# A decoder layer on one core: both layernorm quarters between the halves of the output's products

## The chip, the cores and the metric

The kernel runs on one core of one Trainium2 chip. The time is the device time of one execution in microseconds (us). A core has five engines that run side by side, each through its own queue in order: TensorE (PE in the profile; its weight loads are listed as PEld), VectorE (DVE), ScalarE (ACT), GpSimd (POOL) and SyncE (SP), which here only issues transfers. An instruction that waits holds back everything behind it in its engine's queue.

## The reference

The input x is 8 batches of 256 rows of 1024 values. The layer is

```
x = x + attn(layernorm(x))          # 32 heads of 32, 8 key/value heads, sign weights
x = x + xattn(layernorm(x), ctx)    # 16 heads, low-rank queries and keys
x = x + ffn(layernorm(x))           # low-rank gate/up and down, silu
```

In the self-attention every projection (q, k, v and the output) is a product with the signs of a weight matrix, scaled per output by the mean of that row's absolute weights and a given factor, and passed through nan_to_num (NaN to 0, infinities to plus or minus 1e6). The scores are softmaxed over 256 keys. All is float32.

## The kernel before, in words

Rows are worked on in tiles of 128, two to a batch (`TB` = 2). The self-attention runs batch by batch in steps: step c (0 to 7) of a batch handles four heads. The cross-attention follows in steps of the same form, then the feed-forward part.

One step, written out by `step` (from L682), does the following, in program order. TensorE makes the scores `s` of four heads (L549) into four PSUM banks of the pool `pss`. VectorE reduces each head's row maximum to `nm` (L692). TensorE transposes the four heads' probabilities of the *step before* in four groups of four (`turned`, L528), each into a PSUM bank from `bank`, and ScalarE copies each group out as `pT` (L532). ScalarE makes the eight exponentials `p` (L711), two to a head, each with its row sum by an accumulator read. At the end TensorE multiplies the turned probabilities with v (`weighted`, L587).

Between the transposes and that last product lie the step's *parts*: pieces of other work that fill TensorE while the softmax is under way. `self_plan(b)` lists the parts for each of the eight steps of batch b, and `run_part` runs one. The parts that matter here are:

- `o_parts`: the output projection of the batch before, one for each row tile and half of the columns. It is a PSUM sum of 16 matmuls (L496) in two halves of 8; after the second half VectorE scales it to `y` (L505), and `nan_to_num` makes `z` and `fin` on VectorE (L355, L358) and `tmp` and a sum on GpSimd (L356, L357). A predicated copy (L361) and the residual sum on GpSimd (L510) follow some parts later.
- `ln_parts`: the layernorm of the next batch, in quarters (row tile and half of the columns). `normed_half` makes `xn` on VectorE ahead of time (L155), four transposes turn it into a PSUM bank (L163), ScalarE copies it as the rounded high part `xh` (L348), and VectorE subtracts to get the rest `xl` (L349), which frees the bank.
- `lnx_parts`: the same for the cross-attention; VectorE alone copies the bank out as `xT` (L847).

Each part has an estimated duration (2.0 for a half of products, 0.5 for a quarter), and `step` adds these up to place the exponentials between the parts on ScalarE: before each part it issues exponentials while their own count (0.49 each) is behind. A row sum becomes a reciprocal on VectorE for two heads at a time (`over_sums`, L562), and the probabilities are divided in place: the letters in `BY` say for each head by whom, D for VectorE (L572, two instructions), P for GpSimd (L565, one) and A for ScalarE (L579, two, issued at the end of the step by `over_sums_end`). ScalarE also rounds the weighted sums to `oh` (L604) at the head of the next step, and VectorE makes the rest `ol` (L608).

`bank` hands out three PSUM banks in turn (one of the pool psB, two of psA). A step with one product and two layernorm quarters takes seven: four turned groups, the product, and the two quarters. So the first turned group of the next step takes the product's bank, the second the first quarter's, the third the second quarter's, and the fourth the first turned group's own, when ScalarE has copied it out.

The order of every engine's queue is the order in which the program issues (a manual schedule). Transfers are issued from SyncE's queue and, for the writes of x1 and x2, from GpSimd's. Deferred work (`later`, `ripe`, `settle`) runs at the start of the following parts, so the number of parts behind a product decides where the predicated copy, the residual sum and the write of x1 (L515) come.

Of the kernel before, what the change touches and what calls it, by code (L numbers as in the profile page):

```python
# [35 lines left out]
def decoder_layer(  # L36
# [25 lines left out]
    B, S, E = x.shape  # L62
# [261 lines left out]
    def scale_part(col0, n, dst, soon=False):  # L324

        box = {}

        def ahead():
            box["dg"] = wk_.tile([P, n, P], F32, tag="xn", name="dg", bufs=2)
            for k in range(n):  # L330
                nc.gpsimd.tensor_scalar_mul(
                    box["dg"][:, k, :], ident, scol[:, col0 + k : col0 + k + 1]
                )

        def main():
            ps = bank([P, n, P], "ps_d")
            for k in range(n):
                nc.tensor.matmul(ps[:, k, :], ones, box["dg"][:, k, :], start=True, stop=True)
            nc.vector.tensor_copy(dst, ps.rearrange("p k c -> p (k c)"))

        return Part(0.3 * n, main, ahead, soon)

    def weight(i):
        return Part(1.1, lambda: weight_next(i))
# [22 lines left out]
    def ln_parts(st, b):  # L367


        def ahead(q):  # L370
            t, h = q // 2, q % 2
            need(st)
            st.xn = getattr(st, "xn", {})
            st.xn[q] = normed_half(xb[b][t], st.mv[:, t, 0:1], st.rs[:, t : t + 1], h)

        def main(q):
            t, h = q // 2, q % 2
            if q == 0:
                st.xh = wk_.tile([P, EC, S], F32R, tag="xh", name="xh")
                st.xl = wk_.tile([P, EC, S], F32R, tag="xl", name="xl")  # L380
            ps = four_T(st.xn.pop(q), "ps_t")
            e4, t4 = slice(h * 4, (h + 1) * 4), slice(t * P, (t + 1) * P)
            split(st.xh[:, e4, t4], st.xl[:, e4, t4], ps)

        return [Part(0.5, lambda q=q: main(q), lambda q=q: ahead(q), True) for q in range(2 * TB)]
# [56 lines left out]
    def q_parts(st, c0):  # L442
        return proj_T(
            st, lambda i, e: qT_w[c0 + i][:, e, :], c0, lambda: st.qT[:, c0 : c0 + 2, :]
        )
# [3 lines left out]
    def k_parts(st):  # L449
        def dst():  # L450
            st.kT = wk_.tile([P, 2, S], F32, tag="kT", name="kT", bufs=2)
            st.qT = wk_.tile([P, EC, S], F32, tag="qT", name="qT", bufs=2)
            return st.kT

        def then():
            nc.vector.tensor_scalar_mul(st.kT, st.kT, K_SCALE)

        return proj_T(st, lambda i, e: kT_w[:, e, i * P : (i + 1) * P], 8, dst, then)

    def v_parts(st):  # L460
        box = {}

        def main(t):
            if t == 0:
                box["ps"] = bank([P, TB, KVD], "ps_v")
                box["y"] = wk_.tile([P, TB, KVD], F32, tag="y", name="y", bufs=2)
            ps, y = box["ps"], box["y"]
            for e in range(EC):
                for x_ in (st.xh, st.xl):
                    nc.tensor.matmul(  # L470
                        ps[:, t, :],
                        x_[:, e, t * P : (t + 1) * P],
                        vT_w[:, e, :],
                        start=(e == 0 and x_ is st.xh),
                        stop=(e == EC - 1 and x_ is st.xl),
                    )
            if t == TB - 1:
                for k in range(TB):
                    nc.vector.tensor_mul(y[:, k, :], ps[:, k, :], v_sc)
                st.v = wk_.tile([P, TB, KVD], F32, tag="v", name="v", bufs=2)  # L480
                nan_to_num(st.v, y, [P, TB, KVD], None)

        return [Part(2.0, lambda t=t: main(t)) for t in range(TB)]
# [306 lines left out]
    def ctx_parts(st, copies):  # L790
        def main(q):
            t, h = q // 2, q % 2
            if q == 0:
                st.cT = wk_.tile([P, EC, S], F32, tag="xh", name="cT")
            ps = four_T(st.c[t][:, h * 512 : (h + 1) * 512], "ps_c")
            copies[h](st.cT[:, h * 4 : (h + 1) * 4, t * P : (t + 1) * P], ps)

        return [Part(0.5, lambda q=q: main(q), hold=True) for q in range(2 * TB)]
# [25 lines left out]
    def ckvT_part(st):  # L824
        def main():
            ps = bank([P, TB, XD], "ps_kt")
            for k in range(TB):
                nc.tensor.transpose(
                    ps[:, k, :], st.ckv[0:XD, k * P : (k + 1) * P], ident[0:XD, 0:XD]
                )  # L830
            nc.vector.tensor_copy(st.ckvT, ps)

        return [Part(0.3, main)]

    def lnx_parts(st):
        def ahead(q):
            t, h = q // 2, q % 2
            need(st)
            st.xn = getattr(st, "xn", {})
            st.xn[q] = normed_half(st.x[t], mv2[st.b][:, t, 0:1], rs2[st.b][:, t : t + 1], h)  # L840

        def main(q):
            t, h = q // 2, q % 2
            if q == 0:
                st.xT = wk_.tile([P, EC, S], F32, tag="xl", name="xT")
            ps = four_T(st.xn.pop(q), "ps_t")
            dve(st.xT[:, h * 4 : (h + 1) * 4, t * P : (t + 1) * P], ps)  # L847

        return [Part(0.5, lambda q=q: main(q), lambda q=q: ahead(q), True) for q in range(2 * TB)]

    def cq_part(st):
        def main():
            ps = bank([P, S], "ps_q")
            for e in range(EC):
                nc.tensor.matmul(  # L855
                    ps, xw.wqd[:, e, :], st.xT[:, e, :], start=(e == 0), stop=(e == EC - 1)
                )
            st.cq = wk_.tile([P, S], F32, tag="v", name="cq", bufs=2)
            nc.vector.tensor_scalar_mul(st.cq, ps, 1.0 / 8.0)

        return [Part(3.5, main)]
# [242 lines left out]
    def tail(fb, j):  # L1104
# [16 lines left out]
    BY = {  # L1121
        0: ["DDDD", "PPPD", "PPPD", "PPPP", "PPPD", "PPPD", "DDDD", "PPPD"],
        1: ["DDAA", "PPAA", "PPAA", "DDDA", "DDAA", "DDDA", "DDDA", "DDDA"],
        B - 1: ["DDAA", "DDDA", "DDDA", "PPAA", "PPAA", "DDDA", "DDDA", "DDDA"],
    }
    sts, xts = [], []
    for b in range(B):
# [6 lines left out]
    def mixed(a, b):  # L1134
        out = []
        for i in range(max(len(a), len(b))):
            out += a[i : i + 1] + b[i : i + 1]
        return out

    def o_all(st):  # L1140
        return [o_parts(st, t, h) for t in range(TB) for h in range(2)]

    def self_plan(b):
        st = sts[b]
        if b == 0:
            nxt = sts[1]
            v0 = v_parts(st)
            ln, k, v = ln_parts(nxt, 1), k_parts(nxt), v_parts(nxt)
            return [
                [weight(4), weight(5), v0[0], weight(6), weight(7)]  # L1150
                + [scale_part(10, 2, v_sc), v0[1]],
                mixed(q_parts(st, 2) + q_parts(st, 4), [weight(8), weight(9), weight(10)]),
                [weight(11)] + q_parts(st, 6) + [weight(12)],
                [weight(13)] + ln[:2] + [weight(14)] + ln[2:],
                k[:1] + [weight(15)] + k[1:],
                mixed(v, [weight(16), weight(17)]),
                mixed(q_parts(nxt, 0), [weight(18), scale_part(12, 4, o_sc[:, 0:512], True)])
                + [weight(19)],
                mixed(q_parts(nxt, 2), [scale_part(16, 4, o_sc[:, 512:1024])]),
            ]  # L1160
        o = o_all(sts[b - 1])
        if b + 1 < B:
            nxt = sts[b + 1]
            ln = ln_parts(nxt, b + 1)
            return [
                q_parts(st, 4) + q_parts(st, 6),
                mixed(o[0], ln[:2]),
                mixed(o[1], ln[2:]),
                k_parts(nxt),
                o[2] + v_parts(nxt),  # L1170
                o[3],
                q_parts(nxt, 0),
                q_parts(nxt, 2),
            ]
        x0 = xts[0]
        ln = lnx_parts(x0)
        return [
            q_parts(st, 4) + q_parts(st, 6),
            o[0],
            o[1],  # L1180
            mixed(o[2], ln[:2]),
            mixed(o[3], ln[2:]),
            ctx_parts(x0, (act, dve)) + ckv_part(x0),
            cq_part(x0) + ckvT_part(x0),
            cqk_parts(x0, (dve, act)),
        ]
# [208 lines left out]
```

## Time and profile before

| what | value |
|---|---|
| runs | 1550.12, 1550.95, 1551.24 us; median 1550.95 |
| the profiled execution's own time | 1550.99 us |
| its span in the profile | 1549.2 us |
| granted TensorE clock, mean over the span | 0.997 |
| TensorE busy | 1509.7 us (97%) |
| VectorE busy | 963.9 us (62%) |
| ScalarE busy | 798.3 us (52%) |
| GpSimd busy | 401.5 us (26%) |

Times inside the profile count from the start of the span. Self-attention takes about the first 636 us, in a pattern that repeats every 73.04 us, once a batch; cross-attention and feed-forward follow. A row of the timeline gives start, length, engine, source line, operation, the tiles written and read, their shapes, how many instructions were merged into the row (x4), and in brackets the idle time before it with what ended that. A row of the waits gives the total, how often, and the longest. A step is told by its scores (L549): in the fourth batch those of c=1 start at 284.84, of c=2 at 293.55 and of c=3 at 302.58. Shares of busy time over the whole span are means over parts of the kernel with different limits; the steps in question are looked at by themselves.

### The profile page before, as it was taken

What the parts mean: (1) busy time and instruction counts of PE and PEld (TensorE: products, weight loads), DVE (VectorE), ACT (ScalarE), POOL (GpSimd) and SP (SyncE); (2) the same over time, 40 slices, a digit from 0 to 9 for tenths busy, and PEclk for the clock granted to TensorE, in tenths of its full rate; (3) what the DMA queues carried; (4) which work ended last, traced back from release to release, by engine and by line L of the source; (5) the groups of instructions that cost most, each with busy time, mean ns of one, the idle gap of its engine ahead of it and who ended that gap; (6) DMA issues with size and microseconds to landing.
All of it is one profiled execution on the core that took longest, in us unless ns stands there. A gap on an engine that the chain in (4) does not pass through costs nothing.

```text
span 1549.2 us, 25717 instructions
## 1 busy us (share of the span) xinstructions
PE 1509.7 (97%) x9494; PEld 1014.9 (66%) x9494; DVE 963.9 (62%) x1880; ACT 798.3 (52%) x2448; POOL 401.5 (26%) x475
## 2 busy tenths in 40 slices
PE   6889999999999999999999999999999999999998
PEld 5777788888878787777777777544444444444443
DVE  7888899999999899766676665343233223423322
ACT  4677898989888888755566666311101111111110
POOL 2555454435344545022321111131001100100000
PEclk9999999999999999999999999999999999999999
DMA  8430020101020141211445312110011002000001
GB/s 228 73 83 17 27 69 29 56 29 56 28 69 17 56 144 59 93 42 57 140 156 175 120 48 93 62 41 0 0 48 61 0 3 106 0 1 27 28 0 54
DMA packets 67916, 92.78 MB, mean 60 GB/s; under 512 B 40474, under 2 KB 46416, under 8 KB 67664
## 3 DMA queue, kind: packets, MB, share of 16 engines
q1 hardware_dynamic: 63184, 74.37, 15.4%
q0 software_dynamic: 4608, 16.78, 2.7%
q8 instruction: 75, 1.23, 0.3%
q14 instruction: 49, 0.40, 0.1%
HBM read 65.44 MB, written 25.17 MB: 58 GB/s over the span
## 4 chain that ended last, share of the span: by engine, by line
PE 80%; DVE 10%; ACT 6%; issue 1%; POOL 1%; DMA 1%; SPq 0%; DVEq 0%; ACTq 0%; POOLq 0%
PE ps_h L1045 19%; PE ps_z L1089 9%; PE ps_pt L528 9%; PE ps_q L403 7%; PE ps_o L496 5%; ACT p L711 4%; PE ps_p L1019 4%; PE ps_o L1108 4%; PE s L625 3%; PE po L648 3%; PE s L549 3%; PE po L587 3%; DVE nm L692 2%; PE ps_q L855 2%; PE ps_qk L870 2%; PE ps_v L470 2%
## 5 line engine op out<-in xcount | busy, mean ns | idle before, releaser
L711 ACT ACTIVATE p<-s,nm 128x256 f32<-128x256 f32 x768 | 357.4, 516 | 0.4 <-DVE nm L692 0.4
L532 ACT COPY pT<-ps_pt 128x512 f32<-128x512 f32 x384 | 198.6, 599 | 177.5 <-PE ps_pt L528 176.7
L1057 ACT ACTIVATE sg<-ps_h,b_col 128x512 f32<-128x512 f32 (+1 forms) x88 | 59.6, 677 | 413.5 <-PE ps_h L1045 413.5
L692 DVE TENSOR_REDUCE nm<-s 128x2 f32<-128x512 f32 x384 | 237.5, 679 | 8.4 <-PE s L625 6.0
L1058 DVE SCALAR_TENSOR_TENSOR sg<-ps_h,b_col,sg 128x512 f32<-128x512 f32 (+1 forms) x88 | 65.0, 739 | 273.0 <-ACT sg L1057 273.0
L528 PE MATMUL ps_pt<-ident,p 128*128 128x128 f32 x1536 | 195.7, 278 | 4.9 <-DVE xl L349 3.0
L528 PEld LDWEIGHTS ps_pt<-ident,p 128*128 128x128 f32 x1536 | 164.4, 141 | 45.5 <-issue 25.2
L711 ACT ACTIVATION_READ_ACCUMULATOR p<-s,nm 128x1 f32 x768 | 190.8, 248 | 0.0
L1089 PE MATMUL ps_z<-ac,u_sb 128*128 128x512 f32 x336 | 157.7, 593 | 0.0
L403 PE MATMUL ps_q<-xh,qT_w 128*128 128x256 f32 x496 | 121.8, 287 | 0.0
L403 PE MATMUL ps_q<-xl,qT_w 128*128 128x256 f32 x496 | 118.9, 281 | 0.0
L1345 POOL TENSOR_TENSOR x2t<-x2t,b_sb 128x1024 f32<-128x1024 f32 x16 | 37.6, 2356 | 296.2 <-DVE xn L155 296.2
L680 POOL TENSOR_TENSOR x1t<-x1t,y 128x256 f32<-128x256 f32 x64 | 47.2, 758 | 233.0 <-DVE y L673 230.5
L1089 PEld LDWEIGHTS ps_z<-ac,u_sb 128*128 128x128 f32 x336 | 61.9, 190 | 68.8 <-issue 68.8
L496 PE MATMUL ps_o<-oT_w,oh 128*128 128x512 f32 x256 | 105.8, 413 | 0.0
L356 POOL TENSOR_SCALAR tmp<-y 128x512 f32<-128x512 f32 x78 | 57.3, 734 | 183.9 <-DVE y L505 106.4
L496 PE MATMUL ps_o<-oT_w,ol 128*128 128x512 f32 x256 | 101.0, 394 | 0.0
L572 DVE TENSOR_SCALAR p<-p,sm 128x256 f32<-128x256 f32 x252 | 90.2, 415 | 8.0
L403 PEld LDWEIGHTS ps_q<-xh,qT_w 128*128 128x128 f32 x496 | 93.3, 188 | 1.6
L403 PEld LDWEIGHTS ps_q<-xl,qT_w 128*128 128x128 f32 x496 | 93.4, 188 | 0.0
L1045 PE MATMUL ps_h<-pT,w_ffn 128*128 128x512 f32 (+1 forms) x184 | 88.7, 577 | 0.0
L1045 PE MATMUL ps_h<-late,w_ffn 128*128 128x512 f32 (+1 forms) x184 | 88.7, 577 | 0.0
(159 smaller groups left out, 2737.1 us busy)
## 6 DMA issues: line engine op xcount, KB each, us to landing
xs<-in_x_dram SPq DMA_DIRECT2D x32, 512.0 KB, 4.3
x<-xs POOLq DMA_DIRECT2D x16, 512.0 KB, 3.0
x1t<-x SPq DMA_DIRECT2D x16, 512.0 KB, 6.6
c<-in_ctx_dram SPq DMA_DIRECT2D x16, 512.0 KB, 3.7
x<-x1t POOLq DMA_DIRECT2D x16, 512.0 KB, 3.8
x2t<-x SPq DMA_DIRECT2D x16, 512.0 KB, 5.2
out_dram<-x2t SPq DMA_DIRECT2D x32, 256.0 KB, 2.0
w<-in_L_attn_q_weight_dram SPq DMA_DIRECT2D x32, 128.0 KB, 5.5
```

Source lines behind the costliest of these rows:

```text
L403: nc.tensor.matmul(ps[:, i, :], w(i, e), x_[:, e, :], start=(e == 0 and x_ is st.xh), stop=(e == EC - 1 and x_ is st.xl),)
L496: nc.tensor.matmul(ps, o_[c // 4][:, c % 4, t * P : (t + 1) * P], oT_w[:, c, h * 512 : (h + 1) * 512], start=(c == 0 and o_ is st.oh), sto ...
L528: nc.tensor.transpose(ps[:, k, t * P : (t + 1) * P], p[:, t, k * P : (k + 1) * P], ident)
L532: nc.scalar.copy(pT, ps)
L572: nc.vector.tensor_scalar_mul(p, p, self.sm[:, t, j : j + 1])
L692: nc.vector.tensor_reduce(nm[:, j, :], s[j], AX.X, ALU.max, negate=True)
L711: nc.scalar.activation(cur.p[j][:, t, :], s[j][:, t, :], AF.Exp, bias=nm[:, j, t : t + 1], accum_out=cur.sm[:, t, j : j + 1],)
L1019: nc.tensor.matmul(ps, fw.u1[:, e, r * P : (r + 1) * P], fb.xT[e // 4][:, e % 4, :], start=(e == 0), stop=(e == EC - 1),)
L1045: nc.tensor.matmul(ps[h * n : h * n + n], v1_of(r, i, f, n), fb.pT[:, r, h * w_ : (h + 1) * w_], start=(r == 0), stop=(r == RC - 1),)
L1058: nc.vector.scalar_tensor_tensor(sg[:m], hs[0][:m], bg, sg[:m], ALU.add, ALU.mult)
L1089: nc.tensor.matmul(fb.zs[r], fw.u2[f // 4][:n, f % 4, r * P : (r + 1) * P], ac[:n], start=(k == 0), stop=(k == NF - 1 and COPIES < 2),)
L1108: nc.tensor.matmul(ps, fb.zT[:, r, j * P : (j + 1) * P], fw.v2[:, r, h * 512 : (h + 1) * 512], start=(r == 0), stop=(r == RC - 1),)
```

## The change

In the self-attention steps that hold layernorm quarters (c=1 and c=2 of the second to seventh batch, c=3 and c=4 of the last), the parts were product half, quarter, product half, quarter. Now both quarters stand between the halves. On ScalarE this also moves the second `xh` ahead of the last two exponentials of its step, since exponentials are placed by the parts' estimated durations; on VectorE the second `xl` (or `xT`) moves ahead of the second reciprocal and of `y`, `z` and `fin`. The numbers of instructions on TensorE stay the same.

In step c=2 of the last batch the third head is divided by ScalarE (A) and not by VectorE (D).

Two side effects of the parts' order, both in or behind the last batch: one write of x1 on GpSimd's queue comes ahead of a `tmp` and its sum, not behind them, and in c=7 one pair of statistics instructions on VectorE (L138, L140) comes behind the divisions and a copy, not ahead of them.

```diff
     BY = {
...
-        B - 1: ["DDAA", "DDDA", "DDDA", "PPAA", "PPAA", "DDDA", "DDDA", "DDDA"],
+        B - 1: ["DDAA", "DDDA", "DDAA", "PPAA", "PPAA", "DDDA", "DDDA", "DDDA"],
     }
...
             return [
                 q_parts(st, 4) + q_parts(st, 6),
-                mixed(o[0], ln[:2]),
-                mixed(o[1], ln[2:]),
+                o[0][:1] + ln[:2] + o[0][1:],
+                o[1][:1] + ln[2:] + o[1][1:],
                 k_parts(nxt),
...
             o[0],
             o[1],
-            mixed(o[2], ln[:2]),
-            mixed(o[3], ln[2:]),
+            o[2][:1] + ln[:2] + o[2][1:],
+            o[3][:1] + ln[2:] + o[3][1:],
             ctx_parts(x0, (act, dve)) + ckv_part(x0),
```

`mixed(a, b)` takes one from each list in turn; `ln` has four entries, one for each quarter, and `o[i]` two, one for each half.

## The prediction

> **What bounds the kernel now.** I read the page's busy shares first, then TensorE's waits, then the timelines of all engines over two steps that the change reorders, then those two steps as windows.
>
> ```profile
> PE 1509.7 (97%) x9494; PEld 1014.9 (66%) x9494; DVE 963.9 (62%) x1880; ACT 798.3 (52%) x2448; POOL 401.5 (26%) x475
> ```
>
> TensorE stands still for 39.5 us of 1549.2, much of it at the start. Only waits in the reordered steps are open to this change. TensorE's waits over the whole span hold one row from them:
>
> ```profile
> PE ps_pt L528 <- DVE xl L349: 3.0, 9, 0.4
> ```
>
> That is the third group of probability transposes, held by a PSUM bank that the last xl subtraction of the step before frees. The windows of the steps c=1 and c=2 of the fourth batch say what is close behind:
>
> ```profile
> 287.70:296.70 9.00, 8.84 (x74) 6.67 (x73) 8.11 (x17) 8.66 (x28) 5.29 (x6) 1.00 0.33 117
> 296.70:306.00 9.30, 8.88 (x76) 6.58 (x74) 8.24 (x16) 8.66 (x28) 5.29 (x5) 1.00 0.19 59
> ```
>
> Columns: window, length, busy PE, PEld, DVE, ACT, POOL, clock, DMA share, GB/s. VectorE and ScalarE are over nine tenths busy too, so each must be followed. The timeline of TensorE in c=2 and at the head of c=3:
>
> ```profile
> 298.73 0.63 PE L163 MATMUL ps_t<-ident,xn 128*128 128x128 f32 x4
> 299.11 0.48 PE L496 MATMUL ps_o<-oT_w,oh 128*128 128x512 f32 x1
> ...
> 301.05 0.60 PE L163 MATMUL ps_t<-ident,xn 128*128 128x128 f32 x4
> 301.58 1.07 PE L587 MATMUL po<-pT,v 128*32 128x256 f32 x16
> 302.58 1.15 PE L549 MATMUL s<-kT,qT 32*128 32x256 f32 x16
> 303.66 1.10 PE L528 MATMUL ps_pt<-ident,p 128*128 128x128 f32 x8
> 305.18 1.06 PE L528 MATMUL ps_pt<-ident,p 128*128 128x128 f32 x8 [0.42 <-DVE xl L349]
> 306.00 0.37 PE L403 MATMUL ps_q<-xh,kT_w 128*128 128x256 f32 x1
> ```
>
> VectorE's timeline there shows why xl is late: z and fin stretch (0.43 alone, as at 319.27), and xl and nm queue behind them.
>
> ```profile
> 298.84 0.53 DVE L155 TENSOR_SCALAR xn<-xs,mv,rs 128x512 f32<-128x512 f32 x1
> ...
> 301.89 0.66 DVE L505 TENSOR_TENSOR y<-ps_o,o_sc 128x512 f32<-128x512 f32 x1
> 302.58 1.10 DVE L355 TENSOR_SCALAR z<-y 128x512 f32<-128x512 f32 x1
> 303.60 0.83 DVE L358 TENSOR_SCALAR fin<-y 128x512 uint8<-128x512 f32 x1
> 304.36 0.67 DVE L349 TENSOR_TENSOR xl<-ps_t,xh 128x512 fp32r<-128x512 f32 x1
> 304.96 2.47 DVE L692 TENSOR_REDUCE nm<-s 128x2 f32<-128x512 f32 x4
> ```
>
> GpSimd's timeline over the same time:
>
> ```profile
> 301.35 2.05 POOL L565 TENSOR_TENSOR p<-p,sm 128x512 f32<-128x512 f32 x2
> 303.48 0.67 POOL L356 TENSOR_SCALAR tmp<-y 128x512 f32<-128x512 f32 x1
> ```
>
> The divisions end at 303.40 and z at 303.68; tmp ends at 304.15 and fin at 304.43. In c=1 z ends at 294.39 (divisions 294.10) and fin at 295.14 (tmp 294.86). So z and fin end 0.28 us after the GpSimd instruction beside them, whenever they started.
>
> **The change part by part, on the fourth batch.** The layernorm quarters of a step are called ln0 and ln1, the product's halves h0 and h1. Before: h0, ln0, h1, ln1; after: h0, ln0, ln1, h1.
>
> *TensorE's own work: zero.* Gaps at the joints before: into ln0 0.24, ln0 0.36, the first matmul of h1 0.31, into ln1 0.24, ln1 before the weighted products 0.53: 1.68. After: 0.24, ln0 at the pace of 16 transposes in 1.82 (four: 0.46), ln1 0.36, 0.31, and product to weighted products 0.32 (329.07 to 329.39): 1.69. Bounds 0.1 a step either way; I take 0.
>
> *ScalarE.* The second xh (L348) now stands ahead of the last two exponentials, which start 0.47 later (290.77 to 291.24 is one xh). The second reciprocal needs the eighth exponential, and ScalarE's four divisions (L579) need that reciprocal; before, the xh covered this, and now there is the 0.25 gap that a step without layernorm shows (318.44 to 318.69). A step of ScalarE with no other wait is then: to the last accumulate's end 4.74, gap 0.25, four divisions 1.60, oh 0.31, four pT copies 1.91: 8.81. Before, from first exponential to first exponential: 8.99 (288.52 to 297.51) and 9.29 (to 306.80). If ScalarE sets the pace, two steps fall from 18.28 to 17.62: 0.66 less.
>
> *VectorE.* xl leaves the end of the step. y waits for the later reciprocal and ends at 294.05, not 293.58; but the divisions on GpSimd still end at 294.10 and tmp at 294.86 to 294.95 (0.67 alone, 0.77 beside a z), so fin ends 0.28 after that, at 295.14 to 295.23, as before. With no xl behind it nm starts near 295.1, not 295.66: 0.55 earlier. The bounds of this term are 0.13 (y, z and fin all move by the 0.47, and xl's 0.60 is saved) and 0.60.
>
> *The added wait.* ln1 needs the second xn (L155), 298.84 to 299.37 in c=2, plus the 0.15 from xn's end to the transposes (298.58 to 298.73). Behind ln1 on TensorE stand h1 and everything after; on ScalarE the xh that reads ln1 stands ahead of two exponentials, the divisions and the pT copies. With nm 0.55 earlier xn is usable at 298.97.
>
> *TensorE's walk.* In c=2 the third group is free of xl; the fourth waits for the first pT copy's bank to 296.05 (arrival 295.98), h0 for the second's to 296.55 (before: 296.70). ln0 at 298.49, ln1 at 298.97 (0.03 late), h1 at 299.35, weighted products at 301.37 (h1 from start to them 2.02), transposes at 303.45, end at 305.27 if unheld. ScalarE by its own sum has the second pT copy done, and the bank free, at 305.36. So c=3's projection starts at 305.36, not 306.00: 0.64 saved, now set by ScalarE. The score banks are free in time: the eighth exponential ends at 293.2, scores start at 293.55.
>
> *Over the batches.* The third to seventh batch show the same waits: 5 x 0.64 = 3.2. The second batch's c=1 has no wait (8.67 on ScalarE) and loses 0.15, its c=2 gains: 17.95 to 17.62, 0.3.
>
> *The joint (last batch).* In c=2 one head's two divisions leave VectorE (0.62 at 593.00) for ScalarE (two more at 0.40). VectorE's xn and nm come 0.53 earlier; ScalarE's pT copies come at 594.84, not 594.31, and the next h0 at 595.96, not 595.43. That eats most of the wait of 0.85 for xn at 598.42: ln0 at 597.90, ln1 held by the second xn to 598.68, weighted products at 601.08, not 601.29. After c=4 (xT copies on VectorE, none on ScalarE) the saving is 0.24; the 0.85 wait at 616.89 can shrink, but a ScalarE copy at 616.52 stands close behind. I take 0.3; bounds 0.6 lost and 1.1 gained. The x1 write's issue (0.67 on GpSimd) goes ahead of one tmp; its reader, the predicated copy at 607.71, has 2.3 us to spare: 0. One pair of statistics moves behind divisions in c=7: nobody waits there: 0. SyncE's queue is unchanged.
>
> *Sum:* 3.2 + 0.3 + 0.3 = 3.8 from the profiled execution's 1550.99 (span 1549.2 and 1.8 around it): **1547.2**. The runs' median, 1550.95, stands 0.04 below that execution.
>
> **The rivals.**
>
> *A, half the gain.* If z and fin are only slowed beside GpSimd and not held until it ends, they move with y, and nm is 0.13 earlier: xn is usable at 299.39, ln1 waits 0.34 in c=2, and a batch saves 0.31: 5 x 0.31 + 0.2 + 0.25 = 2.0, 1549.0. For it: the z of c=1, 0.77 long, can be read as plain slowing. Against: z began 0.48 before the divisions' end in c=1 and 0.82 before it in c=2, and ended 0.28 or 0.29 behind it both times. The Trainium skill ("GPSIMD Engine Reference", Key points) speaks of contention of GpSimd with VectorE instructions in a two-port mode or with two SBUF inputs, and does not say that one waits out the other; read as mere sharing it gives A's 1549.0, while the trace's 0.28 bears out holding.
>
> *B, no change.* The wait for xl is replaced by one for ScalarE's pT copies at the same transposes; at 222.84 and 514.95 the trace already names pT there (0.20 and 0.19). This needs ScalarE's step to stay at 9.14 on average, 0.33 above my sum: 1551.0.
>
> *C, slower.* ScalarE stands at the second xh because ln1 is late, with two exponentials, four divisions and four copies behind it. ln1 would have to come over 0.55 late in c=2 (its xh is due at 300.54, ln1's output at 299.6 to 300.0). From a wait of 0.33 a step the change loses; at 0.63, below the 0.85 that the joint shows for xn, 12 steps x 0.3 = 3.6: 1554.6. Against: in c=1 xn is ready at 289.79, before ln0 is through (290.07).
>
> **How the numbers follow.** Forecast 0.55 (own range 1545.5 to 1548.2), A 0.24, B 0.11, C 0.10. The lower end is all waits gone: 3.0, 0.4 under pT's name, 0.4 at ln0 (0.09 in each of five batches), and the joint's two 0.85: 5.5. The upper end takes in A and B: 1545.5 to 1551.2. About 0.2%, 3.1 us, is what a measurement of this kernel can tell; 1547.85 lies inside the forecast's range, so most of it, 0.47 in all, is faster; the rest with A and B, 0.43, is the same; C, 0.10, slower.
>
> **What would show it.** Right: no TensorE wait for xl; ScalarE's c=1 and c=2 at about 8.8 each; nm 0.5 earlier; z and fin still ending 0.28 behind GpSimd. Wrong: a wait of 0.2 or more of ln1 for xn in c=2 (A), waits for pT of 0.3 (B), or ScalarE idle before xh (C).

## The result and the profile after

| | before | after |
|---|---|---|
| median of 12 runs, us | 1550.61 (1550.12 to 1551.43) | 1546.57 (1545.86 to 1548.34) |
| ratio to before, 95% interval | | 0.9975, 0.9967 to 0.9982 |
| profiled execution: own time, span | 1550.99, 1549.2 | 1546.57, 1544.8 |

The change makes the kernel 4.0 us faster, a quarter of a per cent; the interval of the ratio leaves out 1. The page's busy times after, to be held against the line of before:

```profile
PE 1511.1 (98%) x9494; PEld 1015.2 (66%) x9494; DVE 956.7 (62%) x1878; ACT 799.2 (52%) x2450; POOL 402.8 (26%) x475
```

TensorE's work is nearly unchanged; VectorE lost 7 us of busy time with two instructions fewer, which says that other instructions became shorter. TensorE's waits over the whole span no longer hold a row of the probability transposes (L528) for xl, and these are the rows nearest to it:

```profile
PE ps_t L163 <- DVE xn L155: 2.9, 3, 2.3
...
PE ps_pt L528 <- ACT pT L532: 0.8, 2, 0.5
```

The fourth batch again, TensorE in c=2 and at the head of c=3:

```profile
295.12 0.50 PE L496 MATMUL ps_o<-oT_w,oh 128*128 128x512 f32 x1
...
297.08 1.22 PE L163 MATMUL ps_t<-ident,xn 128*128 128x128 f32 x8
...
300.09 1.07 PE L587 MATMUL po<-pT,v 128*32 128x256 f32 x16
...
302.17 1.99 PE L528 MATMUL ps_pt<-ident,p 128*128 128x128 f32 x16
303.99 0.39 PE L403 MATMUL ps_q<-xh,kT_w 128*128 128x256 f32 x1
```

The sixteen probability transposes of c=3 now run through in 1.99, where before 0.42 lay between the second and the third group. From the first product half of c=1 (287.73 before, 286.33 after) to c=3's projection (306.00, 303.99) the time fell from 18.27 to 17.66. The eight layernorm transposes take 1.22 here; those of c=1 take 1.04. VectorE over the same time:

```profile
296.99 0.54 DVE L155 TENSOR_SCALAR xn<-xs,mv,rs 128x512 f32<-128x512 f32 x1
...
300.80 0.66 DVE L505 TENSOR_TENSOR y<-ps_o,o_sc 128x512 f32<-128x512 f32 x1
301.50 0.43 DVE L355 TENSOR_SCALAR z<-y 128x512 f32<-128x512 f32 x1
301.84 0.84 DVE L358 TENSOR_SCALAR fin<-y 128x512 uint8<-128x512 f32 x1
302.60 2.47 DVE L692 TENSOR_REDUCE nm<-s 128x2 f32<-128x512 f32 x4
```

z is 0.43 long, not 1.10, and no xl lies between fin and nm. GpSimd beside it:

```profile
299.50 2.05 POOL L565 TENSOR_TENSOR p<-p,sm 128x512 f32<-128x512 f32 x2
301.63 0.76 POOL L356 TENSOR_SCALAR tmp<-y 128x512 f32<-128x512 f32 x1
```

The divisions end at 301.55, too early to hold z; tmp ends at 302.39 and fin at 302.68, 0.29 behind it. tmp in its turn ends 0.46 behind z, which ends at 301.93; before, these were 304.15 and 303.68, 0.47 apart.

ScalarE's steps, from first exponential to first exponential, take 8.79 (287.12 to 295.91) and 8.86 (to 304.77), before 8.99 and 9.29.

Where the time went, counted on the starts of every step's scores (time saved against before):

| stage | saved, us |
|---|---|
| second batch, c=1 to c=4 | 0.26 |
| third to seventh batch, c=1 to c=4 | 0.61, 0.58, 0.54, 0.55, 0.60 |
| last batch, c=3 to c=5 | 0.41 |
| cross-attention, two steps | 0.24, 0.35 |

These add up to 4.1. Each kernel's steps are read from one profiled execution; self-attention steps behind the start-up that no edit touches agree there within 0.1. The start-up part, up to the second batch, is up to 2.4 us longer and 1.4 us shorter in the profiled executions below than in that of before, and is left out of such sums.

### The profile page after: what moved, and what is told of

It is laid out like the page before. It is cut to its first block, busy times and chain, and to the rows that moved or that the text cites. A ratio compares the mean times of both kernels' runs of the same rounds, so it can differ in the third digit from the quotient of the medians.

```text
span 1544.8 us, 25713 instructions
## 1 busy us (share of the span) xinstructions
PE 1511.1 (98%) x9494; PEld 1015.2 (66%) x9494; DVE 956.7 (62%) x1878; ACT 799.2 (52%) x2450; POOL 402.8 (26%) x475
## 4 chain that ended last, share of the span: by engine, by line
PE 88%; DVE 5%; ACT 3%; DMA 2%; POOL 1%; issue 1%; SPq 0%; DVEq 0%; ACTq 0%; POOLq 0%
PE ps_h L1045 19%; PE ps_pt L528 10%; PE ps_z L1089 9%; PE ps_q L403 8%; PE ps_o L496 7%; PE s L549 4%; PE po L587 4%; PE ps_p L1019 4%; PE ps_o L1108 4%; PE s L625 3%; PE po L648 3%; PE ps_q L855 2%; PE ps_qk L870 2%; PE ps_t L163 2%; PE ps_o L665 2%; PE ps_v L470 2%
## 5 line engine op out<-in xcount | busy, mean ns | idle before, releaser
L528 PE MATMUL ps_pt<-ident,p 128*128 128x128 f32 x1536 | 194.6, 279 | 1.8 <-DVE o_sc L339 1.0
L528 PEld LDWEIGHTS ps_pt<-ident,p 128*128 128x128 f32 x1536 | 164.3, 141 | 41.5 <-issue 26.6
```

The source lines that it names most:

```text
L528: nc.tensor.transpose(ps[:, k, t * P : (t + 1) * P], p[:, t, k * P : (k + 1) * P], ident)
```

## The experiments

The theory of the prediction: z and fin wait for the GpSimd instruction beside them, xl and nm queue behind, and with xl out of there ScalarE sets the step. Its rivals were mere sharing between the engines (A), a wait for pT in place of the one for xl (B), and a loss at ln1 (C). All runs below were timed beside the kernel before, whose medians there were 1550.4 to 1550.7.

**The two halves of the change.** The order in the batches alone:

```diff
-                mixed(o[0], ln[:2]),
-                mixed(o[1], ln[2:]),
+                o[0][:1] + ln[:2] + o[0][1:],
+                o[1][:1] + ln[2:] + o[1][1:],
```

> Only the steps c=1 and c=2 of the second to seventh batch are reordered; the last batch is as before. Theory (the gain is the wait for xl and what stood behind it, batch by batch): these steps save 0.57 us in each of five batches and 0.26 in the second, as in the trace of the changed kernel, so 3.1 us less than before, near 1547.5; TensorE's wait list has no row for xl at the transposes of L528. Rival (the gain sits in the last batch's division and in the cross-attention behind it): 1 us less or nothing, and the step table shows the saving only after c=3 of the last batch.

Measured: 1547.44 (1546.71 to 1548.41), ratio 0.9978 (0.9969 to 0.9987). The batches save 0.26 and 0.59 to 0.61; the last batch and cross-attention save nothing.

The joint alone (the last batch's order and its division, nothing else):

```diff
-        B - 1: ["DDAA", "DDDA", "DDDA", "PPAA", "PPAA", "DDDA", "DDDA", "DDDA"],
+        B - 1: ["DDAA", "DDDA", "DDAA", "PPAA", "PPAA", "DDDA", "DDDA", "DDDA"],
...
-            mixed(o[2], ln[:2]),
-            mixed(o[3], ln[2:]),
+            o[2][:1] + ln[:2] + o[2][1:],
+            o[3][:1] + ln[2:] + o[3][1:],
```

> Only the last batch is changed, order and division; the other batches are as before. Theory: the weighted products of c=3 and all behind them come 0.4 us earlier, and the xl waits of the other batches stay at 3.0 in all; 1550.2. Rival: 1.0 us or more, with the cross-attention's 0.6 among it (the changed kernel's trace has 0.24 and 0.35 in the second batch's cross-attention, which no edit touches); 1549.6 or less.

Measured: 1549.89, ratio 0.9994 (0.9986 to 1.0003): by time alone not told from no change. By the steps: 0.41 in the last batch, 0.23 and 0.35 in cross-attention, none in the batches. So the rival had it right by the steps: cross-attention's 0.6 comes with the last batch's changes. The two halves add up to the whole.

**One step at a time.** Only c=1 in the new order:

```diff
-                mixed(o[0], ln[:2]),
+                o[0][:1] + ln[:2] + o[0][1:],
```

> Only c=1 of the second to seventh batch is reordered. Theory (VectorE's row maxima come 0.55 earlier in c=2, GpSimd's divisions there too, and z and fin end 0.28 behind GpSimd): in c=2 the old order keeps its xl at the end, but xl is done 0.3 earlier; about 0.33 a batch in five batches: 1.7 us less, 1548.9. Rival (only the order within c=2 counts, where the longer wait of 0.42 is): 0.15 a batch at most, 1549.9, and the wait for xl at the head of c=3 stays at 0.4.

Measured: 1548.84, ratio 0.9988 (0.9979 to 0.9996); 0.10 and then 0.44 to 0.47 a batch, more than the 0.33 expected. With c=1 alone, c=2's own late xl and ScalarE's copies remain, and TensorE waits for pT instead:

```profile
PE ps_pt L528 <- ACT pT L532: 2.1, 7, 0.5
```

This is rival B's wait, and it takes only a part back. Only c=2 in the new order:

```diff
-                mixed(o[1], ln[2:]),
+                o[1][:1] + ln[2:] + o[1][1:],
```

> Only c=2 of the second to seventh batch is reordered. Theory (the second quarter's xn is late unless c=1 is reordered too): ln1 waits about 0.34 us for xn in c=2 of every batch, the wait of 0.42 for xl goes, and 0.2 a batch is left: 1.2 us less, 1549.4; TensorE's list shows ps_t waiting for xn, six times about 0.3. Rival (xn is early enough, the wait for xl is all that counts): 0.42 a batch, 2.5 us less, 1548.1, no wait for xn.

Measured: 1549.82, ratio 0.9992 (0.9984 to 1.0001): by time alone not told from no change; by the steps, 0.15 to 0.22 a batch. In the fourth batch the second xn ends at 298.32 and ln1 starts at 298.47, 0.33 behind the end of ln0's four transposes at their pace of 0.46: without c=1's earlier nm the quarters stand too early for xn. (The list of waits puts these down to ScalarE's p, not to xn; but the 0.15 from xn's end to ln1's start is the same as in the prediction's 298.58 to 298.73.) C put the point from which nothing is gained at a wait of 0.33 a step; with 0.33 in c=2 alone, a smaller gain was left.

**The joint's two parts.** The division alone:

```diff
-        B - 1: ["DDAA", "DDDA", "DDDA", "PPAA", "PPAA", "DDDA", "DDDA", "DDDA"],
+        B - 1: ["DDAA", "DDDA", "DDAA", "PPAA", "PPAA", "DDDA", "DDDA", "DDDA"],
```

> Only the third head's division in c=2 of the last batch goes from VectorE to ScalarE; every order is as before. Theory (the division is what shortens the wait of 0.85 for xn in c=3): the weighted products of c=3 come 0.5 us earlier. The 0.24 and 0.35 that the last batch's changes also saved in the cross-attention: if they hang on the number of instructions (two fewer on VectorE, two more on ScalarE), they appear here, 1.1 in all, 1549.5; if they hang on the order, only 0.5, 1550.1. Rival (the order saves it): 0.1 or less.

Measured: 1549.52, ratio 0.9995 (0.9986 to 1.0003), not told from no change by time alone. By the steps it saves 0.54 up to the scores of c=4 and loses 0.39 on the way to c=5, and it alone brings the 0.23 and 0.35 of cross-attention. The loss is the same hold as in the batches, VectorE in c=3 of the last batch, with GpSimd's divisions beside it:

```profile
599.94 1.32 DVE L355 TENSOR_SCALAR z<-y 128x512 f32<-128x512 f32 x1
601.19 0.83 DVE L358 TENSOR_SCALAR fin<-y 128x512 uint8<-128x512 f32 x1
```

```profile
598.94 2.05 POOL L565 TENSOR_TENSOR p<-p,sm 128x512 f32<-128x512 f32 x2
601.07 0.67 POOL L356 TENSOR_SCALAR tmp<-y 128x512 f32<-128x512 f32 x1
```

y came earlier, so z met the divisions from their middle on and stood until 601.26, 0.27 behind their end. The order alone:

```diff
-            mixed(o[2], ln[:2]),
-            mixed(o[3], ln[2:]),
+            o[2][:1] + ln[:2] + o[2][1:],
+            o[3][:1] + ln[2:] + o[3][1:],
```

> Only the order in c=3 and c=4 of the last batch is changed; the division stays on VectorE. Theory: xn for the first quarter is as late as before (598.42 in the span of before), and ln1, right behind it, waits for the second xn to 599.21, so c=3's weighted products come 0.3 us later and stay so: 1550.9. Rival (the order is the gain): 0.4 earlier, 1550.2.

Measured: 1550.9, ratio 1.0002 (0.9993 to 1.0011), again not told from no change by time; by the steps 0.35 is lost up to the scores of c=4. ln1 starts there at 597.84, 0.33 behind the end of ln0's transposes at their pace (597.05 and 0.46). So the order loses without the division, and with it turns 0.15 into 0.41.

**Does ScalarE set the pace?** The changed kernel, with the second reciprocal cut in two, so that ScalarE's first divisions need not wait for the eighth exponential:

```diff
-            r = self.sm[:, :, heads[0] : heads[-1] + 1]
-            nc.vector.reciprocal(r, r)
+            both = [heads] if self.by[2:] != "AA" or not pair else [heads[:1], heads[1:]]
+            for hs in both:
+                r = self.sm[:, :, hs[0] : hs[-1] + 1]
+                nc.vector.reciprocal(r, r)
```

> The changed kernel, with the second reciprocal of a step cut in two where ScalarE divides both heads: the third head's as soon as its own sums are there, so that ScalarE goes from the eighth exponential to the first division without the gap of 0.25. Theory (after the change ScalarE's queue sets the pace of c=1 and c=2 at 8.8 us a step, TensorE alone needs 8.55): 0.2 to 0.25 a step, less what the second xn then takes back in c=2; 0.3 to 0.5 a batch, 1.5 to 3 us less than the changed kernel's 1546.6: 1543.6 to 1545.1. Rival (another engine sets the pace, VectorE's row maxima or TensorE itself): no gain, or 0.1 a step lost by the extra instruction on VectorE, 1546.6 to 1547.8.

Measured: 1546.45 (1545.95 to 1547.24), ratio 0.9975 (0.9966 to 0.9985), 0.55 to 0.62 a batch: nothing gained. ScalarE's gap of 0.25 before its divisions did go, and then its pT copies wait for TensorE:

```profile
302.39 2.05 ACT L532 COPY pT<-ps_pt 128x512 f32<-128x512 f32 x4 [0.35 <-PE ps_pt L528]
```

TensorE's layernorm transposes in c=2 start 0.10 earlier against the scores of c=1 (13.55 behind them, 13.65 in the changed kernel) and take 0.08 longer, so that the product's second half starts as late as before:

```profile
296.52 1.30 PE L163 MATMUL ps_t<-ident,xn 128*128 128x128 f32 x8
```

In the changed kernel the fourth group of transposes at the head of c=2 starts 0.11 late, behind the first pT copy (the sixteen take 2.09, not 1.99). The cut reciprocal takes this wait away (1.99 again), and ln1 then waits that much longer for the second xn. So ScalarE does hold TensorE at the head of c=2, but it is not what the time hangs on: that is ln1, which waits for the second xn. z holds tmp, tmp holds fin, fin holds nm, nm holds xn.

**The hold itself.** In the changed kernel, a longer GpSimd instruction beside fin; VectorE's instructions stay the same:

```diff
-        nc.gpsimd.tensor_scalar(tmp, y, 0.0, -1e6, ALU.min, ALU.max)
+        nc.gpsimd.tensor_mul(tmp, y, y)
```

(in the self-attention's output projection only).

> The changed kernel, with a longer GpSimd instruction beside fin in the output projection: in place of tmp, a product y*y into the same tile (the lower clamp is not computed), a two-input instruction like the sum behind it, which takes 1.28 to 1.34, where tmp took 0.76 to 0.83. VectorE's instructions stay the same. Theory 1 (fin waits until the GpSimd instruction beside it ends, and ends 0.28 behind it): in the fourth batch's c=2 the product runs from 301.63 to about 302.95, fin is 1.4 long and not 0.83, nm and the second xn come 0.55 to 0.6 later in c=1 and in c=2, ln1 waits for xn, and a batch loses one to two of these: the 0.58 that a batch saved against the kernel before is gone or turned round. About 1550 to 1553. Theory 2 (two instructions that share a port and slow each other): fin already lies wholly beside GpSimd's work and its 0.83 is twice its 0.41, so that a longer neighbour changes nothing: fin stays at 0.83, the time at 1546.6.

Measured: 1552.34 (1552.09 to 1553.39), ratio 1.0013 (1.0004 to 1.0022). Fourth batch, c=2, VectorE, GpSimd and ln1 on TensorE:

```profile
303.71 1.26 DVE L361 TENSOR_SCALAR fin<-y 128x512 uint8<-128x512 f32 x1
```

```profile
303.47 1.22 POOL L359 TENSOR_TENSOR tmp<-y 128x512 f32<-128x512 f32 x1
```

```profile
299.61 0.63 PE L163 MATMUL ps_t<-ident,xn 128*128 128x128 f32 x4 [0.16 <-DVE xn L155]
```

GpSimd's product ends at 304.69 and fin at 304.97, 0.28 behind it; in c=1 it is 295.55 and 295.83. Sharing (theory 2) left fin at 0.83; it is 1.26 here. ln1 in c=2 starts 0.33 behind the end of ln0's transposes at their pace (298.82 and 0.46). The saving of a batch falls from 0.58 to about 0.13, the second batch loses 0.21, the last batch's joint loses 1.40, and three steps of cross-attention, where the last products are finished, lose 0.43 each. Rival A's mechanism is out.

**The hold taken away.** The kernel before without GpSimd's tmp and sum in the output projection:

```diff
-        nc.gpsimd.tensor_scalar(tmp, y, 0.0, -1e6, ALU.min, ALU.max)
-        nc.gpsimd.tensor_add(dst, dst, tmp)
```

> The kernel before, without the two GpSimd instructions tmp and z+tmp of the output projection's nan_to_num (all of them, also in the last batch); the lower clamp of that projection is left out. Theory (fin runs 0.83 instead of 0.41 because it waits out tmp, and so xl is late): fin takes 0.41, xl ends 0.4 earlier, the waits for xl in c=2 and c=3 go, and the old order is as fast as the new one: 3 us less than before, 1547.6. Rival (xl is late by its place in the order, not by GpSimd): fin stays at 0.83 or xl stays late; less than 1 us gained, above 1549.6.

Measured: 1544.1 (1543.85 to 1544.66), ratio 0.996 (0.9947 to 0.9972), more than was expected and more than the change brought, in the old order: 0.81 to 0.86 a batch (0.50 in the second). VectorE in c=2:

```profile
300.41 0.97 DVE L355 TENSOR_SCALAR z<-y 128x512 f32<-128x512 f32 x1
301.31 0.41 DVE L359 TENSOR_SCALAR fin<-y 128x512 uint8<-128x512 f32 x1
301.64 0.68 DVE L349 TENSOR_TENSOR xl<-ps_t,xh 128x512 fp32r<-128x512 f32 x1
```

z is still held by the divisions; fin is 0.41, and no wait of TensorE for xl is left. The same cut in the changed kernel:

> The changed kernel, with GpSimd's tmp and the sum z + tmp left out in the self-attention's output projection (so the lower clamp of its nan_to_num is not computed). Theory 1, that the new order helps only because it goes round the GpSimd instruction that holds fin: with tmp gone, fin takes 0.41 and nm comes 0.43 earlier; the 0.14 that ln1 still waits for xn goes, and then ScalarE's 8.81 (with its 0.25 gap between the second reciprocal and the divisions) sets the step. A batch saves 0.75 against the kernel before, less than the 0.82 of the old order without tmp; with what the old order without tmp also saved outside these steps, about 1544.5, not below the 1544.1 of the old order without tmp. Theory 2, that order and tmp cost separately: the savings add, 4 and 6.5 us, about 1540.

Measured: 1544.17 (1543.76 to 1545.26), ratio 0.9959 (0.9946 to 0.9971); 0.69 to 0.72 a batch. The savings don't add: with tmp gone the new order brings nothing, and in the batches it is 0.1 behind the old one. Theory 1 had this right.

**A kernel that computes everything, and in which tmp holds nothing.** fin goes first, z second, and GpSimd's tmp takes its zero from a column that VectorE sets behind z, so that it can't start beside either:

```diff
-        nc.vector.tensor_scalar(dst, y, 0.0, 1e6, ALU.max, ALU.min)
-        nc.gpsimd.tensor_scalar(tmp, y, 0.0, -1e6, ALU.min, ALU.max)
-        nc.gpsimd.tensor_add(dst, dst, tmp)
         nc.vector.tensor_scalar(fin, y, 0.0, 0.0, ALU.mult, ALU.is_equal)
+        nc.vector.tensor_scalar(dst, y, 0.0, 1e6, ALU.max, ALU.min)
+        zero = wk_.tile([P, 1], F32, tag="zero", name="zero", bufs=2)
+        nc.vector.memset(zero, 0.0)
+        nc.gpsimd.tensor_scalar(tmp, y, zero, -1e6, ALU.min, ALU.max)
+        nc.gpsimd.tensor_add(dst, dst, tmp)
```

(in the output projection). In the old order:

> The kernel before, whole in what it computes; in the output projection VectorE makes fin first and z second, then sets a column of one element a row to zero, and GpSimd's tmp takes its zero from that column, so that it starts only behind z and can hold neither. Theory 1 (a VectorE instruction of this kind ends 0.28 us after the GpSimd instruction beside it, and tmp is what holds fin): fin is still held by the divisions, to 303.68 in the fourth batch's c=2, z ends 0.43 later, at 304.11, and the column at about 304.2; xl starts there and not at 304.36, in c=1 at 294.9 and not 295.14. With 0.2 a step, 0.4 a batch, and little from the other steps: 1548. Rival, that the time which tmp took is paid behind: tmp and the sum end 1.1 later, the predicated copy waits for the sum and holds VectorE, and nothing or less than nothing is saved: 1550.6 or more.

Measured: **1543.65** (1543.32 to 1544.45), ratio 0.9956 (0.9942 to 0.9969): faster than both kernels, 2.9 us below the changed one. VectorE and GpSimd in c=2 of the fourth batch:

```profile
299.91 0.96 DVE L356 TENSOR_SCALAR fin<-y 128x512 uint8<-128x512 f32 x1
300.80 0.41 DVE L357 TENSOR_SCALAR z<-y 128x512 f32<-128x512 f32 x1
301.14 0.68 DVE L349 TENSOR_TENSOR xl<-ps_t,xh 128x512 fp32r<-128x512 f32 x1
301.16 0.06 DVE L359 MEMSET zero<- 128x1 f32 x1
```

```profile
298.55 2.04 POOL L573 TENSOR_TENSOR p<-p,sm 128x512 f32<-128x512 f32 x2
301.39 0.69 POOL L360 TENSOR_SCALAR tmp<-y,zero 128x512 f32<-128x512 f32 x1 [0.80 <-DVE zero L359]
```

fin is held by the divisions (end 300.59; fin 300.87), z is not held by anything, and the column costs VectorE next to nothing: xl starts 0.34 behind z's start, and in the kernel without tmp 0.33 behind fin's. A batch saves 0.79 to 0.83 (the second 0.51), the last batch 0.78, and three steps of cross-attention, where the last batch's products are finished with the same instructions, 1.27; 0.35 of this is a pause of VectorE that is told of below. The expectation, 0.4 a batch, was too small because it added lengths as they stand in the rows; instructions on one queue start 0.07 before the one ahead ends (300.80 against 300.87), and the column was counted as 0.1. The rival's price is real but hidden: VectorE's predicated copies of z wait 13.6 us for GpSimd's sum over the span, before 7.0, and no step grows by it. In the new order:

> The changed kernel, whole in what it computes, with the same edit: fin, z, the zero column on VectorE, and only then tmp on GpSimd. Theory 1: in c=2 of the fourth batch fin is held by the divisions to 301.83, z ends at 302.26, the column at 302.35, and nm starts there and not at 302.60; the second xn comes 0.25 earlier, ln1's wait of 0.14 for it goes, and a batch saves 0.72 and not 0.58 against the kernel before: 1546.57 less 0.8, about 1545.8. Rival, that the predicated copy now waits for GpSimd's later sum and holds VectorE in the steps that follow: 1547 or more.

Measured: 1544.28 (1544.01 to 1544.87), ratio 0.9959 (0.9947 to 0.9972), 0.66 to 0.69 a batch. That is near the 0.72 expected; the total is 1.5 below the expectation, which left out what the last batch (0.57) and cross-attention (0.93) gain on top of the changed kernel. Here ScalarE does set the pace, with the gap that the prediction named, in c=1 and in c=2:

```profile
291.50 1.71 ACT L587 ACTIVATE p<-p,sm 128x256 f32<-128x256 f32 x4 [0.25 <-DVE sm L570]
...
300.29 1.71 ACT L587 ACTIVATE p<-p,sm 128x256 f32<-128x256 f32 x4 [0.25 <-DVE sm L570]
```

Its steps are 8.79 (300.29 less 291.50; the prediction's sum was 8.81), its copies wait for nothing, and TensorE's step c=2 is 8.78. In the old order, where the second xh covers that gap, the same step is 8.69.

## Why the prediction was right, and where it was not

- *The wait for xl goes, 3.2 + 0.3 in the batches.* Right in cause, a little too large: 2.9 in the third to seventh batch (0.54 to 0.61, not 0.64) and 0.26 in the second. The order in the batches alone brings this, the joint alone none of it. Of the signs that the prediction named, the wait for xl is gone and ScalarE's steps are near 8.8 (8.79 and 8.86); ln1's wait, 0.14, stays below A's 0.2.
- *TensorE's own work: zero.* Right: in c=1, where nothing waits, it takes 4.82 from the product's start to the weighted products before (287.73 to 292.55) and 4.79 after (286.33 to 291.12).
- *z and fin end 0.28 behind the GpSimd instruction beside them.* Right, and the longer instruction shows that it is a hold and no sharing. It also decides against rival A. The Trainium skill ("SBUF — State Buffer", Who interferes with whom) states this outright: VectorE in its two-port mode and GpSimd exclude each other for a whole instruction, and the later one fully blocks. The runs agree, with 0.28 or 0.29 from GpSimd's end to VectorE's, and 0.46 to 0.48 from z's end to tmp's where tmp comes second; which mode z and fin run in, no trace here says. The Trainium skill's "GPSIMD Engine Reference" (Key points), which the prediction weighed, names the contention without that.
- *nm 0.55 earlier.* Measured 0.45: from c=1's first product half to c=2's nm 7.93 before (287.73 to 295.66) and 7.48 after (286.33 to 293.81). The step behind it that was mis-sized is tmp at "0.67 alone, 0.77 beside a z": it was 0.83 in c=1. No length of tmp was right to take, since both of these were held by z as well: tmp ends 0.47 behind z, and takes 0.61 where it starts first (before, at 284.93, in another projection). fin's end follows from z's, 0.75 behind it.
- *ln1 0.03 late in c=2.* Measured 0.14: xn ends at 297.53 and is usable at 297.68, ln0 is through at 297.54 (0.46 after 297.08). It follows from the 0.10 that nm lacks, and is where the 0.06 a batch went.
- *"Now set by ScalarE."* Wrong for c=3's projection, though by little. The two limits stood 0.09 apart in the prediction's walk (305.27 and 305.36), and with ln1 0.11 later than forecast TensorE's own came last: its transposes in c=3 run unheld, and ScalarE's first copy waits 0.07 for them. At the head of c=2 ScalarE did hold TensorE, by 0.11. The cut reciprocal gained nothing; only with tmp tied behind z did ScalarE's 8.8 become the bound.
- *The joint, 0.3.* Measured 0.41, made of terms that the walk did not have apart: 0.54 from the division, 0.39 lost again to z behind the divisions, and an order that loses 0.35 alone and gains 0.26 with the division.
- *Cross-attention: not in the sum.* It gave 0.59 of the 4.1, and this made up for the batches: luck. It comes with the division (its own run shows 0.23 and 0.35). The traces show two short pauses before that are gone after. In the one step ScalarE's four pT copies take 2.28 before and 2.06 after:

```profile
686.09 2.28 ACT L532 COPY pT<-ps_pt 128x512 f32<-128x512 f32 x4 [6.53 <-PE ps_pt L528]
```

```profile
682.06 2.06 ACT L532 COPY pT<-ps_pt 128x512 f32<-128x512 f32 x4 [6.53 <-PE ps_pt L528]
```

  In the other, VectorE's y of one product starts 0.44 after the product's last matmul ends (715.73), and 0.09 after it with the change, with nothing else named:

```profile
716.17 0.69 DVE L505 TENSOR_TENSOR y<-ps_o,o_sc 128x512 f32<-128x512 f32 x1 [3.70 <-PE ps_o L496]
```

```profile
711.55 0.69 DVE L505 TENSOR_TENSOR y<-ps_o,o_sc 128x512 f32<-128x512 f32 x1 [3.34 <-PE ps_o L496]
```

  Each pause goes with the length of its own engine's queue, and not with any order or with what the other engines do. ScalarE's stands at this place in all six kernels whose ScalarE queue has as many records in the trace, its waits counted, as before (3006). In the old order without tmp, which has 3000, it stands nine steps later, and in the other seven kernels cross-attention shows none. VectorE's stands in the five kernels whose VectorE queue has 2214 records, and in none of the other nine. By this, the division helped here because it moved two instructions from one queue to the other, some 100 us earlier. That is read from the traces and was not tested, and what makes the pauses stays open.
- *Rivals.* B's wait for pT grows most where c=1 alone is changed (to 2.1 us in all, from 0.9). C did not come in the changed kernel: ln1 waits, but 0.14, short of the 0.33 a step from which C had the change lose. Its loss shows where the last batch's order is changed without the division: ln1 0.33 late, and 0.35 lost. With c=2 alone, or with the longer instruction, ln1 is 0.33 late in c=2 only, and the third to seventh batch still save 0.11 to 0.22 each.

So the total was right partly by luck: the batches came out 0.4 below the forecast (3.1 against 3.5), the joint 0.1 above it, and cross-attention, which the forecast did not have, gave 0.6.

## What to carry to other kernels

When an element-wise VectorE instruction is longer in one place than in another, look at what GpSimd does beside it: if the two end a fixed time apart wherever they meet, as here, it is a hold, and what queues behind on VectorE pays for it. Taking the hold away by a dependency of one column was worth 7 us here; steering the order of the work round it was worth 4, and the two don't add. Where two limits come out within 0.1 of one another, name both: which of them binds is not known until one is moved.

## What the runs showed of the hardware that was not expected

- The hold works on VectorE's instruction with uint8 output too: fin takes 0.41 to 0.43 alone, 0.83 or 0.84 beside tmp, up to 1.26 beside divisions or the product y*y, ending 0.28 or 0.29 behind. In the kernel before, from 110 us on, 67 z and fin start while a GpSimd instruction is under way and has more than 0.15 to go; all of them end 0.28 or 0.29 behind it.
- It works the other way too: a tmp that starts beside a z ends 0.46 to 0.48 behind z's end, whatever its own length comes to (0.67 before, 0.83 and 0.76 in the changed kernel's c=1 and c=2); the product y*y ends 0.90 behind it. Where no such VectorE instruction is under way at its start, tmp takes 0.61 (before, at 284.93), or 0.69 with its zero from a column.
- Reductions and subtractions that read PSUM are not held: xl takes 0.68 and nm 2.47 with tmp or a sum beside them, as without.
- ScalarE and VectorE each show a pause in cross-attention, 0.23 and 0.35, that moves or goes when its own queue is a few instructions shorter or longer.
